# A graph attention layer on one core: first stage in another order with more row buffers, and an end with scores pair by pair

## The chip, the core and the metric

The kernel runs on one core of a Trainium2 chip. The metric is the time of one execution on the device, in microseconds, lower is better. The core has five engines that run beside each other, each through its own list of instructions in order: TensorE (PE; its weight loads are shown as PEld), VectorE (DVE), ScalarE (ACT), GpSimd (POOL) and SyncE (SP), which here only issues DMAs. ACT and POOL issue DMAs too.

## The reference

One layer of a graph network with 12,500 nodes, 212,500 edges sorted by their destination, 128 features and 8 heads of 16. The layernorm has no scale and no offset:

```python
h0 = maximum(layernorm(x), 0)
q = (h0 @ Wq.T + bq).reshape(N, 8, 16)
k = (edge_attr @ Wk.T + bk).reshape(-1, 8, 16)
v = (h0 @ Wv.T + bv).reshape(N, 8, 16)
qs, qd = q[src], q[dst]
in_m, out_m, diag_m = sum(qs * k, -1), sum(qd * k, -1), sum(qs * qd, -1)
score = (segment_softmax(in_m * SCALE, dst) + segment_softmax(out_m * SCALE, dst)
         + segment_softmax(diag_m * SCALE, dst)) * edge_weight ** lam
h = segment_sum(score[..., None] * v[dst], dst)
out = x + leaky_relu(h.reshape(N, 128) @ Wo.T + bo, 0.1)
```

Since v depends on the destination alone, the scores are summed for each node first, and v is multiplied once per node.

## The kernel before

**First stage.** x is held in SBUF as 98 tiles of 128 nodes (`xq`), loaded in runs by SP. It is worked off in 25 turns of four tiles: DVE measures (`bn_stats`, L897, then five small operations for the sums, L903 to L908), ACT takes the root (L912), DVE inverts (L916, L917), ACT rectifies (L927), PE turns the tile (L934), ACT copies it (L936), PE multiplies by Wq (L942), DVE adds the bias (L945), and SP stores q to a table in DRAM (L946), `q_table`. For eight of the 25 turns a split of q in three bf16 terms is made here and stored as well (a second view of the same table): `term_1` casts (ACT, L957), `less_1` subtracts it from q in place (DVE, L960), `term_2` casts the rest (ACT, L963), `term_3` subtracts again (DVE, L967). The other 17 turns' terms are made in the main loop, where the rest is formed by two matmuls (L1514, L1515). A dictionary `side` puts other small jobs on turns: the destinations' conversion and differences (`cast_dst`, `mark`, `edges_3`), weights (`turn_ws`), and so on. Every instruction's place on its engine is fixed by the program's own order (`pin`).

**Rows of the sources.** Edges are in 416 blocks of 512: five streams, with 83 groups of one block each, plus a short last one of 20 edges ("few"). Each block needs q of 512 source nodes, gathered by POOL with four indirect DMAs into a buffer `qq` of which there are `QQ` = 22. For the first 20 blocks (`RAW`) it gathers rows of x instead, which need no finished table, and the layernorm and the product with Wq are done on the gathered rows (`raw_measure` with `bn_stats` at L981, `raw_rectify` L714, and the rest in the first stage for `SOON` = 4 blocks, in the loop for the others, with a bias add at L1561). The later blocks gather from `q_table` (L702), which must be whole. `LOOK` = 20 is how many blocks ahead the loop gathers; the first three from the table, and then the rows of the few (`gather_few`, L730), are issued before the loop.

**Main loop.** Per block: PE turns the edge features (L1222), multiplies by Wk (L1229, L1231), spreads q of the destination nodes by a one-hot matrix (L1239); ACT copies (L1224, L1242); DVE makes three products (L1250 to L1252) and reduces to logits (L1253). `logits_few` (L1291 to L1307) does the same for the short block, at the seventh block. Per group: running maxima by scans on DVE (L1313 to L1343), powers (L1363, L1364), a product with the weights (L1375), and `to_rows`: sums of the powers per destination, by PE with a selection matrix (L1403), copied by ACT (L1408) and put into the `sums` tables in DRAM by SP (`put_rows`, L1419). `to_rows` handles three streams in one matmul: 126 columns of weights, 144 moving, of which the three blocks on the diagonal are used; eight of them per group. Edge features come by one DMA of 1280 KB per group (`fetch_edges`), in two buffers.

**Nodes and the end.** Behind the blocks, pairs of units of 256 nodes are finished: `scores` (L1112 to L1118, among them a reciprocal), `weigh` by v (L1178), the product with Wo (L1168, L1170), x added (L1194, L1195), the result stored (L1201). After the last block the remaining scans, powers and rows follow, then the remaining pairs (`rest`, five of them): their sums are loaded (L1143 on SP, L1145 on ACT), second parts added (L1732), scores made for all in one go over 432 columns, and then each pair is weighed, projected and stored.

Of the kernel before, what the change touches and what calls it, by code (L numbers as in the profile page):

```python
# [472 lines left out]
def ordered_path(ctx: ExitStack, tc: tile.TileContext, flag, x, src, dst, edge_attr, edge_weight,  # L473
# [143 lines left out]
    LOOK, QQ, RAW, SOON, DRAIN = 20, 22, 20, 4, 12  # L617
    FIRST, REST = 3, 5
    AHEAD, IDX = LOOK + FIRST, 7
# [31 lines left out]
    def fetch(t):  # L651
# [5 lines left out]
        if t < G:  # L657
# [7 lines left out]
        _, base_v[t] = nc.values_load_multi_w_load_instructions(  # L665
            places[0:1, t, 0:S], engines=[mybir.EngineType.SP], min_val=0, max_val=N - 1,
            skip_runtime_bounds_check_because="the indices of nodes are below N")
        st[t] = dict(relb=relb, far=far)
# [10 lines left out]
    def fetch_edges(t):  # L679
        if t < G:  # L680
            ea = eas[t] = load.tile([P, S, JN * F], F32, name="ea")
            pin(nc.sync.dma_start(
                ea, edge_attr[:end * BE, :].rearrange("(s b p j) f -> p s b (j f)", s=S, b=G, p=P)
                [:, :, t, :]))
# [62 lines left out]

    with tc.tile_pool(name="prep", bufs=1) as prep, \
# [5 lines left out]
        pin(nc.sync.dma_start(lam_sb, lam[None, :].to_broadcast([RW, 1])))  # L754
        w_in = prep.tile([P, 4, F], F32, name="w_in")
        pin(nc.sync.dma_start(w_in[:, 0, :], Wq))
        load_sources(0)
# [25 lines left out]
        for t in range(1, 3):  # L783
            load_sources(t)
        load_x(runs[2:])
        for t in range(3, IDX):
            load_sources(t)
        rows_in(weight, edge_weight.rearrange("e o -> (e o)"), nc.sync)
        b_row = prep.tile([1, 3, F], F32, name="b_row")
        for i, b in enumerate((bv, bk, bo)):  # L790
            pin(nc.sync.dma_start(b_row[:, i, :], b[None, :]))
# [3 lines left out]
        for s in range(S):  # L795
            at = s * G * BE
            pin(nc.sync.dma_start(bases[:, :, s:s + 1], dst[None, at:at + G * BE + 1:BE, None]))
# [13 lines left out]
        for i, w in enumerate((Wv, Wk, Wo)):  # L811
            pin(nc.scalar.dma_start(w_in[:, i + 1, :], w))
# [19 lines left out]
        def of_tile():  # L832
            return prep.tile([P, RC], BF, name="of", tag="of", bufs=2)[:RW]
# [22 lines left out]
        def edges_3():  # L856
            base_c = prep.tile([RW, RB], F32, name="base_c")
            pin(nc.vector.tensor_copy(base_c, dst_f[:, 1:RC + 1:BE]))
            rel_b = got["rel_b"] = of_tile().rearrange("r (a e) -> r a e", a=RB)
            for a in range(RB):  # L860
# [30 lines left out]

        def statistics(rows, *to):

            n = len(rows)
            stats = node.tile([P, CH, 6], F32, name="stats", bufs=1)[:, :n]
            for i, row in enumerate(rows):
                pin(nc.vector.bn_stats(stats[:, i, :], row))  # L897
            return sum_up(stats, n, *to)

        def sum_up(stats, n, *to):  # L900
            sums3 = node.tile([P, 3, CH], F32, name="sums3", bufs=4)[:, :, :n]
            total, apart, sq = sums3[:, 0], sums3[:, 1], sums3[:, 2]
            pin(nc.vector.tensor_add(total, stats[:, :, 1], stats[:, :, 4]))  # L903
            pin(nc.vector.tensor_sub(apart, stats[:, :, 1], stats[:, :, 4]))
            pin(nc.vector.tensor_add(sq, stats[:, :, 2], stats[:, :, 5]))
            pin(nc.vector.scalar_tensor_tensor(apart, apart, F / 4.0, apart, op0=ALU.mult,
                                               op1=ALU.mult))
            pin(nc.vector.tensor_add(sq, sq, apart))  # L908
            return *to, total, sq
# [166 lines left out]
        for g in range(-2, GN):  # L1076
# [9 lines left out]
            if g == -2:  # L1086
                for of in range(RAW):
                    gather(of)
# [702 lines left out]
```

## Time and profile before

| | |
|---|---|
| time, median of three executions | 2201.93 us (2199.54 to 2204.43) |
| profiled execution, its own time | 2203.34 us |
| its span in the profile | 2201.5 us |
| granted TensorE clock, mean | 0.796 |
| DVE busy | 2050.1 us, 93% |
| PE busy | 1779.5 us, 81% |
| POOL busy | 1586.5 us, 72% |
| ACT busy | 1372.0 us, 62% |
| DMA | 355.66 MB, 162 GB/s in the mean |

In rows of the timeline, the first number is the start in microseconds from the start of the span, the second the time busy; then engine, line, operation, output and inputs, how many were merged into the row, and in brackets how long the engine had been idle and what ended that. An engine's name with a q (SPq) is an issue of a DMA. In rows of groups, the columns after the bar are busy microseconds, mean nanoseconds of one, and idle time ahead with what ended it.

### The profile page before, as it was taken

How to read it: one execution, taken by the hardware profiler on the slowest of the kernel's cores; microseconds unless marked ns; L12 is line 12 of the kernel's file. 1: busy time of each engine (PE TensorE's matmuls, PEld its weight loads, DVE VectorE, ACT ScalarE, POOL GpSimd, SP SyncE). 2: the span in 40 equal slices, each digit the busy share in tenths (PEclk: the TensorE clock that was granted, in tenths of full speed). 3: DMA queues.
4: the chain of work that ended last, by engine and by line, in shares of the span. 5: the costliest groups of instructions: out<-in, count | busy, mean ns of one | idle time of the engine just before them, and what ended most of it. 6: DMA issues, size and time to landing. Idle time of an engine off the chain costs nothing.

```text
span 2201.5 us, 36690 instructions
## 1 busy us (share of the span) xinstructions
PE 1779.5 (81%) x10812; PEld 1418.5 (64%) x10812; DVE 2050.1 (93%) x2893; ACT 1372.0 (62%) x2555; POOL 1586.5 (72%) x1676
## 2 busy tenths in 40 slices
PE   4677888877887888888888888888888978888785
PEld 2565766666666666666766766766666767666664
DVE  6877999999999999999999999999999999999994
ACT  4777656665666566666656666666666656666671
POOL 7746777777777777777777777777777777777750
PEclk8788778787788778877878787787878787787887
DMA  8585456556646555655555565565555555555531
GB/s 227 168 252 159 145 150 181 158 162 177 169 148 189 165 161 154 187 162 164 157 169 154 144 186 149 156 171 151 151 167 162 154 170 155 150 171 158 156 99 58
DMA packets 373744, 355.66 MB, mean 162 GB/s; under 512 B 187698, under 2 KB 293437, under 8 KB 373327
## 3 DMA queue, kind: packets, MB, share of 16 engines
q1 hardware_dynamic: 304493, 237.91, 37.1%
q0 software_dynamic: 53184, 108.92, 17.8%
q10 hardware_dynamic: 15856, 6.39, 1.2%
q8 instruction: 87, 1.43, 0.3%
q14 instruction: 124, 1.02, 0.2%
HBM read 320.83 MB, written 32.17 MB: 160 GB/s over the span
## 4 chain that ended last, share of the span: by engine, by line
DVE 50%; PE 14%; DMA 11%; issue 4%; ACT 3%; POOL 1%; DVEq 1%; SPq 0%; ACTq 0%; POOLq 0%
DVE lT L1253 18%; DMA qq<-q_table,sources 11%; DVE prod L1250 7%; DVE prod L1252 7%; DVE prod L1251 7%; DVE m L1343 4%; PE k_ps L1231 4%; DVE l_ps L1313 3%; PE w_ps L1403 2%; PE eT_ps L1222 2%; DVE back L1363 1%; POOL qq L702 1%; PE m_ps L1355 1%; PE k_ps L1229 1%; DVE back L1375 1%
## 5 line engine op out<-in xcount | busy, mean ns | idle before, releaser
L702 POOL DMA_INDIRECT qq<-q_table,sources x1580 | 1498.2, 948 | 520.1 <-issue 219.1
L1253 DVE TENSOR_REDUCE lT<-prod 128x96 f32<-128x1536 f32 x415 | 727.4, 1753 | 14.3
L1231 PEld LDWEIGHTS k_ps<-wk,eT 128*128 128x128 f32 x3320 | 505.6, 233 | 201.2 <-issue 199.9
L1231 PE MATMUL k_ps<-wk,eT 128*128 128x128 f32 x3320 | 597.2, 335 | 0.7 <-ACT eT L1224 0.7
L1242 ACT COPY qd<-qd_ps 128x512 f32<-128x512 f32 x415 | 244.4, 589 | 138.7 <-DVE prod L1252 133.3
L1222 PE MATMUL eT_ps<-ident,ea 128*128 128x128 f32 x1660 | 310.3, 319 | 18.5 <-ACT eT L1224 16.1
L1364 ACT ACTIVATE back<-back 128x480 f32<-128x480 f32 x83 | 50.1, 604 | 416.8 <-DVE back L1363 416.8
L693 ACT ACTIVATE relb<-relb,before 126x512 bf16<-126x512 bf16 x415 | 303.4, 731 | 0.0
L1250 DVE TENSOR_TENSOR prod<-qq,qd_ps 128x512 f32<-128x512 f32 x412 | 279.0, 677 | 14.6 <-ACT qd L1242 9.1
L1239 PE MATMUL qd_ps<-win,oh 126*128 126x128 bf16 x1660 | 189.5, 245 | 124.2 <-DVE prod L1250 95.4
L1252 DVE TENSOR_TENSOR prod<-qd,k_ps 128x512 f32<-128x512 f32 x415 | 281.7, 679 | 0.0
L1251 DVE TENSOR_TENSOR prod<-qq,k_ps 128x512 f32<-128x512 f32 x412 | 279.7, 679 | 0.0
L1224 ACT COPY eT<-eT_ps 128x512 f32<-128x512 f32 x415 | 239.7, 578 | 62.6 <-PE eT_ps L1222 53.6
L1222 PEld LDWEIGHTS eT_ps<-ident,ea 128*128 128x128 f32 x1660 | 232.6, 165 | 60.0 <-ACT eT L1224 41.6
L694 ACT ACTIVATE oh<-relb 126x512 bf16<-126x512 bf16 x415 | 261.4, 630 | 13.2
L1239 PEld LDWEIGHTS <-oh 126*128 126x128 bf16 x1660 | 151.9, 112 | 148.2 <-issue 138.2
L1229 PE MATMUL k_ps<-b,ones 3*128 3x512 bf16 x415 | 186.7, 450 | 73.0 <-DVE prod L1252 70.9
L1403 PE MATMUL w_ps<-back,sel 128*126 128x144 f32 (+1 forms) x1344 | 212.6, 319 | 28.0 <-ACT sel L1393 12.6
L1403 PEld LDWEIGHTS w_ps<-back,sel 128*126 128x126 f32 (+1 forms) x1344 | 202.3, 219 | 34.4 <-ACT sel L1393 15.8
L1355 PE MATMUL m_ps<-ident,m 120*128 120x120 f32 x332 | 83.4, 400 | 85.4 <-DVE m L1343 80.8
L1355 PEld LDWEIGHTS m_ps<-ident,m 120*128 120x128 f32 x332 | 56.4, 217 | 104.1 <-DVE m L1343 67.4
L1343 DVE TENSOR_TENSOR_SCAN m<-far,head,l_ps 120x512 f32<-120x512 bf16 x81 | 102.9, 1271 | 0.0
(222 smaller groups left out, 1770.1 us busy)
## 6 DMA issues: line engine op xcount, KB each, us to landing
ea<-in_edge_attr_dram SPq DMA_DIRECT2D x83, 1280.0 KB
relb<-rel_d SPq DMA_DIRECT2D x83, 630.0 KB
qq<-q_table,sources POOLq DMA_INDIRECT x1580
win<-q_table SPq DMA_DIRECT2D x415, 31.5 KB
far<-far_d SPq DMA_DIRECT2D x84, 120.2 KB
q_table<-q SPq DMA_DIRECT2D x24, 384.0 KB
sums<-rows SPq DMA_DIRECT2D x412, 7.9 KB
q_table<-xq SPq DMA_DIRECT2D x24, 256.0 KB
```

Of the source, the lines that this page charges most:

```text
L693: pin(nc.scalar.activation(d, d, AF.Abs, bias=before[:K3]))
L694: pin(nc.scalar.activation(oh, d, AF.Relu, bias=1.0, scale=-1.0))
L702: rows = pin(nc.gpsimd.indirect_dma_start(out=qq[:, j, :], out_offset=None, in_=x if g < RAW else q_table, in_offset=bass.IndirectOffsetOn ...
L1222: pin(nc.tensor.transpose(eT_ps[:, j, :], eas[g // S][:, g % S, j * F:(j + 1) * F], ident))
L1231: pin(nc.tensor.matmul(k_ps[:, j, :], eTs[g][:, j, :], wk, start=False, stop=(j == JN - 1)))
L1239: pin(nc.tensor.matmul(qd_ps[:, j, :], ohs[g][:, j * P:(j + 1) * P], d["win"][:, s, :], start=(j == 0), stop=(j == JN - 1)))
L1242: pin(nc.scalar.copy(qds[g], qd_ps))
L1250: pin(nc.vector.tensor_mul(prod[:, :, 1, :], qqs[g], q_ps[g]))
L1251: pin(nc.vector.tensor_mul(prod[:, :, 0, :], qqs[g], ks[g]))
L1252: pin(nc.vector.tensor_mul(prod[:, :, 2, :], qds[g], ks[g]))
L1253: pin(nc.vector.tensor_reduce(lTs[t][:, :, s, :], prod.rearrange("p j i (h d) -> p j (i h) d", d=DIM), AX.X, ALU.add))
L1403: pin(nc.tensor.matmul(w_ps[:, i].rearrange("p s c -> p (s c)"), d["sel"][:n, j, lo:lo + 3, :].rearrange("p s w -> p (s w)"), d["back"][:n ...
```

## The change

It edits four places.

- **Buffers and order of loads.** `LOOK` 20 to 26, `QQ` 22 to 28, `SOON` 4 to 3, `IDX` 7 to 8; `RAW` stays at 20, so nine blocks (36 gathers) and not three are gathered from the table ahead of the few's rows and the loop. Edge features come by block (256 KB) into six buffers. SP loads x first, then the destinations, then the rest; Wv, Wk and Wo move from ACT's to SP's queue, biases, bases and index loads become jobs on turns. The tile `of` has one buffer in place of two.
- **First stage.** The sums take four operations in place of five; measuring is spread evenly, six `bn_stats` a turn; jobs move to other turns (`cast_dst` from turn -1 to 1). The raw rows are measured four blocks at a time; the last four (blocks 16 to 19) in the main loop. `less_1` is gone: the rest of q is formed by PE in PSUM.
- **to_rows.** One matmul for each stream and tile: 20 per group, 42 columns of weights and 48 moving; the copy by ACT is 42 x 240.
- **The end.** Scans, powers and rows of the last three groups interleaved; the last group's rows are put by ACT's queue; sums loaded in merged DMAs (SP for the first parts, ACT for the second); second parts added by DVE for the first pair and by POOL for the others; scores pair by pair, each followed by its weighing and projection.

```diff
-    LOOK, QQ, RAW, SOON, DRAIN = 20, 22, 20, 4, 12
+    LOOK, QQ, RAW, SOON, DRAIN = 26, 28, 20, 3, 12
-    AHEAD, IDX = LOOK + FIRST, 7
+    AHEAD, IDX, EDGES = LOOK + FIRST, 8, 6
...
-    def fetch_edges(t):
-        if t < G:
-            ea = eas[t] = load.tile([P, S, JN * F], F32, name="ea")
+    def fetch_edges(g):
+        if g < end:
+            ea = eas[g] = load.tile([P, JN * F], F32, name="ea", bufs=EDGES)
...
         load_x(runs[:1])
+        load_sources(0)
+        load_x(runs[1:2])
         pin(nc.sync.dma_start(bq_all, bq[None, :].to_broadcast([P, F])))
-        load_x(runs[1:2])
+        load_x(runs[2:8])
+        load_sources(1)
+        load_x(runs[8:])
         rows_in(dst_r[:, 1:RC + 1], dst, nc.sync)
...
-            return prep.tile([P, RC], BF, name="of", tag="of", bufs=2)[:RW]
+            return prep.tile([P, RC], BF, name="of", tag="of")[:RW]
...
-        def less_1(i):
-            pin(nc.vector.tensor_sub(q_of(i), q_of(i), q3s[i][:, :, 0, :]))
-
         def term_2(i):
-            pin(nc.scalar.copy(q3s[i][:, :, 1, :], q_of(i)))
+            rest = rests[i] = prep_ps.tile([P, JN, F], F32, name="t_ps")
+            pin(nc.tensor.matmul(rest, ident, q_of(i), start=True, stop=False))
+            pin(nc.tensor.matmul(rest, minus_b, q3s[i][:, :, 0, :], start=False, stop=True))
+            pin(nc.scalar.copy(q3s[i][:, :, 1, :], rest))
...
             if g == -2:
-                for of in range(RAW):
+                for of in range(3 * S):
                     gather(of)
             aside(g)
             if g == 9:
                 fetch_few()
+                for of in range(3 * S, RAW):
+                    gather(of)
         for g in range(RAW, AHEAD):
             gather(g)
         gather_few()
...
-            w_ps = small([3 * W, 2, 3, 2 * H3], "w_ps")
-            for i, (lo, _) in enumerate(trios):
+            w_ps = small([W, S, 2 * H3], "w_ps")
+            for s in range(S):
                 for j in range(JN):
-                    pin(nc.tensor.matmul(w_ps[:, i].rearrange("p s c -> p (s c)"),
-                                         d["sel"][:n, j, lo:lo + 3, :].rearrange("p s w -> p (s w)"),
-                                         d["back"][:n, j, lo:lo + 3].rearrange("p s i c -> p (s i c)"),
-                                         start=(i == 0 and j == 0), stop=(i == 1 and j == JN - 1)))
+                    pin(nc.tensor.matmul(w_ps[:, s, :], d["sel"][:n, j, s, :],
+                                         d["back"][j][:n, s].rearrange("p i c -> p (i c)"),
+                                         start=(s == 0 and j == 0), stop=(s == S - 1 and j == JN - 1)))
...
+            raw_last(g - 3)
             raw_add(g + SOON - 2)
             raw_product(g + SOON - 1)
...
-        scores_of(ab, score[:, :ab.shape[1]])
...
-                rest[r].weigh(rest[r].held)
+                scores_of(ends_ab[:, r * JN:r * JN + of.n], of.score[:, :of.n])
+                of.weigh(of.held)
+                of.turn(small([P, JN, P], "node_ps"))
+                of.project_o(of.held)
```

`raw_last(g)` takes, for g from 0 to 3, four `bn_stats` of one of the last four raw blocks; at 4 the sums and the root, at 5 the inversion.

More of the change, by code (lines that the diff above doesn't have):

```diff
@@ L1724, in ordered_path @@
         last_pair.turn(small([P, JN, P], "node_ps"))
+        hold(rest[0], "eT_ps")
         last_pair.project_o(small([P, JN, F], "node_ps"))
+        for which, q in ((0, nc.sync), (1, nc.scalar)):
+            for r, of in enumerate(rest):
+                of.load_last(ends_ab[:, r * JN:r * JN + of.n] if which == 0 else of.more, q, which)
+        for of, name in zip(rest[1:], ("k_ps", "qd_ps", "qd_ps", "k_ps")):
+            hold(of, name)
         last_pair.add_x(nc.vector)
         last_pair.store()
-        ab = ends_ab[:, :sum(of.n for of in rest)]
+        score = scan.tile([P, len(rest) * JN, HEADS], F32, name="end_score", bufs=1)
@@ L1742, in ordered_path @@
             if 0 <= r - 2:
-                rest[r - 2].project_o(small([P, JN, F], "node_ps"))
                 rest[r - 2].add_x(nc.vector)
```

316 lines of the change are left out of this document (170 added, 146 removed).

## The prediction

> **What bounds the kernel now.** I read the windows first, cut at the kernel's own stages: 54.6 us is where the sixth turn of the first stage starts, 134.7 where the loop over blocks does its first product, 2137.9 where its last reduce ends.
>
> ```profile
> core 0: us, PE busy (x) PEld busy (x) DVE busy (x) ACT busy (x) POOL busy (x), PEclk, DMA share, GB/s
> 0.00:54.60 54.60, 22.41 (x83) 16.24 (x83) 32.94 (x160) 22.13 (x54) 41.59 (x47) 0.83 0.86 227
> 54.60:134.70 80.10, 53.58 (x291) 43.02 (x292) 62.88 (x230) 58.14 (x139) 41.37 (x43) 0.80 0.60 186
> 134.70:2137.90 2003.20, 1664.63 (x10246) 1329.71 (x10246) 1924.82 (x2458) 1276.39 (x2335) 1503.52 (x1588) 0.80 0.57 162
> 2137.90:2201.50 63.60, 38.93 (x196) 29.54 (x194) 29.52 (x48) 15.34 (x28) 0.00 (x0) 0.69 0.18 55
> ```
>
> The loop is VectorE's (DVE): 1924.8 of 2003.2 us, 96%. Per group of five blocks it takes 2003.2 / 83 = 24.1 us. The other 198 us belong to no engine: in the first window the DMA engines are the busiest (0.86), in the second and the last every engine has holes. The edit is mostly in these three windows.
>
> Second, GpSimd's (POOL's) gathers in the timeline, and the one row of the waits that tells whether DVE wants them:
>
> ```profile
> 134.31 0.94 POOL L702 DMA_INDIRECT qq<-q_table,sources  x1 [26.24 <-DMA win<-q_table]
> 135.56 0.94 POOL L702 DMA_INDIRECT qq<-q_table,sources  x1 [0.30 <-issue]
> ...
> 149.29 0.89 POOL L730 DMA_INDIRECT qq<-q_table,few_i  x1 [0.30 <-issue]
> ...
> 2130.28 0.95 POOL L702 DMA_INDIRECT qq<-q_table,sources  x1 [0.30 <-issue]
> DVE prod L1250 <- DMA qq<-q_table,sources: 0.6, 2, 0.4
> ```
>
> One gather starts every 1.25 us. 395 or 396 blocks of four are 1975-1980 us of gathers; the stretch from 134.31 to 2131.2 is 1997, so POOL idled some 20 us in it. DVE waited 0.6 us for rows in the whole run. POOL starts 20 blocks ahead and ends nearly level (last gather 2131.2, last reduce 2137.9): it is close to being the bound, yet it isn't.
>
> Third, the first stage's timelines: what kept it from starting.
>
> ```profile
> 8.88 0.87 DVE L897 BATCH_NORM_STATS2 stats<-xq 128x6 f32<-128x128 f32 x4 [2.25 <-DMA xq<-in_x_dram]
> 16.04 0.87 DVE L897 BATCH_NORM_STATS2 stats<-xq 128x6 f32<-128x128 f32 x4 [4.87 <-DMA xq<-in_x_dram]
> 50.68 0.69 DVE L960 TENSOR_TENSOR xq<-xq,q 128x512 f32<-128x512 f32 x1 [8.71 <-DMA q_table<-xq]
> 21.33 1.88 ACT L849 CAST dst_r<-dst_r 104x2049 f32<-104x2049 int32 x1
> 27.08 1.63 ACT L927 ACTIVATE xq<-xq,shift,inv 128x128 f32<-128x128 f32 x4
> 37.01 1.64 ACT L927 ACTIVATE xq<-xq,shift,inv 128x128 f32<-128x128 f32 x4
> 40.01 1.66 ACT L927 ACTIVATE xq<-xq,shift,inv 128x128 f32<-128x128 f32 x4
> 54.67 1.63 ACT L927 ACTIVATE xq<-xq,shift,inv 128x128 f32<-128x128 f32 x4
> 47.89 2.19 SPq L946 DMA_DIRECT2D q_table<-xq  x4
> ```
>
> Rectifies that follow one another are 3.0 us apart (37.01, 40.01). The three steps from the third (27.08) to the sixth (54.67) take 27.6 us, 18.6 more than that: x had come late before them (4.87), ACT's and DVE's steps for dst and raw rows lie between (27.08 to 37.01), and at 40.01 all stops. There less_1 (L960) writes its result over q in xq, so it waits until that q is stored; its store was issued at 47.89 only, behind all loads of SP's queue.
>
> **First stage, forecast -18 us (from -8 to -27).** x goes first now. x is 12500 x 128 x 4 = 6.4 MB. The first window ran 227 GB/s at a share of 0.86, so 264 GB/s is my estimate of what the queues can carry; the raw gathers take 128 x 512 B per 1.25 us, 52 of that. 6.4 MB / 212 GB/s = 30 us. dst stands behind x and takes 0.85 MB / 212 = 4 us more if it gets no share before. ScalarE's (ACT's) cast of dst stands in order after the third rectify, so it begins at 30 to 34 and lasts 1.9; three rectifies on, at 3.0 apart, the sixth is at 38 to 42 and not at 54.7: 13 to 17 us, 15 taken.
>
> The other 80.1 us keep their chain of turns. Out go less_1 (8 x 0.6 = 4.8 us of DVE), the statistics of raw blocks 16 to 19 (below, 4.2), some 2 us of sums in fewer calls and the waits on q's stores. In come 16 matmuls for the rest of q:
>
> ```profile
> L1514 PE MATMUL rest_ps<-q_in,ident 128*128 128x512 f32 (+1 forms) x34 | 28.2, 929 | 0.0
> L1515 PE MATMUL rest_ps<-q,minus_b 128*128 128x512 bf16 (+1 forms) x17 | 9.0, 527 | 0.0
> ```
>
> Each rest is two records of the first row (its starts are about 0.5 apart) and one of the second, 1.0 + 0.4 = 1.4 us; 8 are 11 us on TensorE (PE), whose 53.6 us become 65 of 80. DVE falls from 62.9 to 52. There is one new wait: dst's `of` tile has one buffer and not two, so edges_3 on DVE waits for the store of `far`, which is queued on SP behind two stores of q; behind it stand that turn's add of the bias, its statistics, and ACT's next rectify. The 8.71 above is the nearest row, 3 to 5 us my guess. Work gone 11, of which about half was on the chain (DVE was 79% busy), less 3: a gain of 3. Sum -18, the loop starts at 116 or 117. The upper bound of the gain has 15 + 12; the lower has 13 and a loss of 5 to PE.
>
> **Loop, forecast +11 (from +3 to +20).** gather_few is moved behind nine blocks of gathers (36) and not three (12). What waits for its rows:
>
> ```profile
> 171.03 1.75 DVE L1253 TENSOR_REDUCE lT<-prod 128x96 f32<-128x1536 f32 x1
> 175.49 0.47 DVE L1299 TENSOR_TENSOR few_prod<-qq,few_ps 20x128 f32<-20x128 f32 x2 [2.71 <-DMA qq<-q_table,sources]
> 51.29 0.86 DVE L981 BATCH_NORM_STATS2 raw_stats<-qq 128x6 f32<-128x128 f32 x4
> 52.19 0.17 DVE L903 TENSOR_TENSOR sums<-raw_stats 128x8 f32<-128x8 f32 x1
> ```
>
> Before, DVE ends the reduce at 172.78, 38 us after the first gather, and waits 2.7. Now the few rows are asked for 36 x 1.25 = 45 us after it, take 2.4 for two gathers and some 2.5 to land: 50. DVE gets there at 38 plus 3 x 0.87 of the moved statistics, plus the 2.7: about 44. It stops for 6; nothing of the block's later work passes it, since each engine's order is fixed. Moved statistics: 4 x 0.87 + 4 x 0.17 + the inversion = 4.5, plus one more bias add (0.6): 5. Sum +11. The lower bound, +3, has the few rows landing 5 us sooner and some statistics in waits; the upper, a stop twice as long and ACT late behind it.
>
> 28 row buffers in place of 22 let POOL run further ahead. DVE waits 0.6 us for rows, so they buy at most that: 0. Edge features go from one 1280 KB DMA per group to five of 256 KB with six buffers. Row for an issue on SP: the four of 47.89 take 2.19, 0.55 each; four more a group are 2.2 us of a queue with gaps, beside puts of rows and loads of windows. The lead falls from a group to five blocks, 24 us: 0, up to +5.
>
> A rule that speaks against it: the Trainium skill, "DMA: Bandwidth & Descriptors", section Measured, asks for at least 1 MiB per DMA, and its fit gives 2.6 us for 256 KB, 5.0 for 1280 KB (estimates), so five cost 13.0 in place of 5.0. The DMA share of 0.57 has room for that in 24.1 us; by the page the sum would have +0 as well, and +8 x 83 only with no lead at all.
>
> The unnamed part is larger: to_rows is 20 narrow matmuls (42 columns of weights, 48 moving) and not 8 wide ones (126 and 144).
>
> ```profile
> 1211.47 2.23 PE L1403 MATMUL w_ps<-back,sel 128*126 128x144 f32 x16
> 1213.53 0.60 PE L1273 MATMUL l_ps<-ident,lT 128*120 128x128 f32 x4
> 1216.13 0.41 PE L1281 MATMUL h_ps<-ident,lT 16*120 16x16 f32 x4
> 1216.46 0.66 PE L1222 MATMUL eT_ps<-ident,ea 128*128 128x128 f32 x4
> PE qd_ps L1239 <- DVE prod L1250: 95.4, 63, 3.6
> PE k_ps L1229 <- DVE prod L1252: 70.9, 96, 0.8
> ```
>
> Starts: 2.06 us for 16 records is 0.129 each; 0.33 for four with 16 columns is 0.082. Between them, 48 columns give 0.094; 40 records take 3.8 us, +1.7 a group. It lies on PE beside DVE's work; PE's waits for DVE are 166.3 / 83 = 2.0 us a group. So 0, and from 0.102 us a record on ((2.06 + 2.0) / 40) DVE starts to wait. The Trainium skill, "TensorE: Matmul & The Clock Gate", section Back-to-back issue gap, has 62 ns a matmul where N is up to 64 and decode is in software: 40 x 0.062 = 2.5 (an estimate). By that the cost is 0 too, and the third case below has next to no chance; the row of 0.082 already contradicts it for matmuls with weight loads, so I keep the case.
>
> **End, forecast -8 (from 0 to -13).**
>
> ```profile
> 2139.75 0.75 DVE L1115 RECIPROCAL ab<-ab 128x96 f32<-128x96 f32 x1
> 2151.31 6.31 PE L1403 MATMUL w_ps<-back,sel 128*126 128x144 f32 x48 [1.19 <-DVE back L1375]
> 2170.35 0.70 DVE L1194 TENSOR_TENSOR node_ps<-h,node_ps 128x512 f32<-128x512 f32 x1 [14.97 <-ACT h L1189]
> 2171.69 1.95 DVE L1732 TENSOR_TENSOR ends_ab<-ends_ab,qq 128x384 f32<-128x384 f32 x4
> 2175.19 2.85 DVE L1115 RECIPROCAL ends_ab<-ends_ab 128x432 f32<-128x432 f32 x1
> 2179.40 0.69 DVE L1178 TENSOR_TENSOR qq<-eT_ps,end_score 128x512 f32<-128x512 f32 x1
> 2185.38 0.70 DVE L1194 TENSOR_TENSOR node_ps<-qq,node_ps 128x512 f32<-128x512 f32 x1 [4.10 <-ACT qq L1189]
> ```
>
> Between 2171.7 and 2179.4, 7.7 us, DVE makes all scores before the first weigh. Pair by pair the first needs one add (0.5) and one set of scores at the small shape, about 1.9 (the reciprocal is 0.75 of it): the first weigh comes 5 us sooner. The other scores fall in part into DVE's next wait (4.10), but cost more calls, which gives back 2 or 3. to_rows begins group by group, and the last group's puts go over ACT's queue while SP's are still landing; merged loads save issues: 3 to 5 of the 15 us. PE's 60 narrow matmuls end no later than the 24 wide. Sum -8.
>
> **Sum.** -18 + 11 - 8 = -15 on the profiled execution's 2203.3 (span 2201.5): 2188.3. It stands 1.4 above the median of the three runs, so 2187.
>
> **Rivals.** Second case: the first stage hardly gains. x may be no sooner (SP's queue was as full) or PE's 11 us decide the turns: -7 + 11 - 5 = -1, 2201. For it: the first window's DMA share is 0.86; against: the 18.6 us between steps aren't x, and the wait of 8.7 loses its cause.
>
> Third case, slower: narrow matmuls price above 0.102 us a record. At the wide row's 0.129, 5.2 us a group exceed the slack by 1.1, x 83 = +91: 2278; at 0.11 it is 0.3 x 83 = +27: 2214. Against it: 16 columns took 0.082.
>
> Fourth case: POOL, not DVE, sets the last third; with a longer lead its 20 idle us go too: 2167. Against it: 0.6 us of waits. That the added row buffers do nothing is in the forecast.
>
> **Chances.** Forecast 0.60, second 0.16, third 0.14, fourth 0.10. The measurement tells 0.2%, 4.4 us: below 2197.5 is faster, above 2206.3 slower. Forecast: 0.58 faster, 0.02 same. Second: 0.04, 0.06, 0.06 slower. Third: 0.01 same, 0.13 slower. Fourth: faster. Sums 0.72, 0.09, 0.19. Range 2168 to 2210: the sums of the bounds on the forecast's side (2172 to 2199 alone), the second case, and the near end of the third.
>
> **What would show it.** Right: first L1250's counterpart near 117, POOL's first gather from q_table just before it; few_prod with a wait of 5 to 9 us; loop of about 2014; w_ps's 40 records in 3.5 to 4.1 us and PE's waits for DVE smaller by 1.7 a group; end of 55. Wrong: the loop starting after 125; DVE waits for qd or k of over 40 us in all; DVE's waits for ea; a loop shorter than 2003.

## The result, and the profile after

The changed kernel takes 2193.85 us (2192.16 to 2194.26, five executions) against 2201.93 for the kernel before in the same comparison (2199.54 to 2204.53): a ratio of 0.9961, 95% interval 0.9950 to 0.9971, some 8 us less. The profiled execution has a span of 2192.1 us, 9.4 less than before.

Six of the runs below were made on two other chips, on which the kernel before took 2717.8 and 2719.3 us; of those only the end of the kernel and the step into the loop are compared with other runs.

The windows of the profile after are cut at the loop's first product and its last reduce, as before; the cut at 41.6, inside the rectifies, only parts the early stretch.

```profile
core 0: us, PE busy (x) PEld busy (x) DVE busy (x) ACT busy (x) POOL busy (x), PEclk, DMA share, GB/s
0.00:41.60 41.60, 13.90 (x46) 9.56 (x47) 17.80 (x86) 14.65 (x33) 30.64 (x38) 0.80 0.92 243
41.60:125.30 83.70, 69.04 (x340) 48.79 (x340) 64.01 (x230) 62.60 (x149) 50.97 (x52) 0.83 0.71 209
125.30:2134.90 2009.60, 1653.25 (x12202) 1310.58 (x12202) 1929.38 (x2481) 1273.09 (x2342) 1502.77 (x1588) 0.80 0.61 162
2134.90:2192.10 57.20, 41.76 (x268) 30.51 (x266) 33.29 (x70) 15.58 (x30) 3.12 (x3) 0.65 0.20 61
```

| stage | before | after | difference | forecast |
|---|---|---|---|---|
| up to the loop's first product | 134.7 | 125.3 | -9.4 | -18 |
| loop | 2003.2 | 2009.6 | +6.4 | +11 |
| after the last reduce | 63.6 | 57.2 | -6.4 | -8 |
| span | 2201.5 | 2192.1 | -9.4 | -15 |

All three signs are as forecast; each size is smaller, the first by half.

**First stage.** ACT's timeline after, at the point where dst is cast:

```profile
16.07 1.64 ACT L932 ACTIVATE xq<-xq,shift,inv 128x128 f32<-128x128 f32 x4
...
37.27 1.90 ACT L879 CAST dst_r<-dst_r 104x2049 f32<-104x2049 int32 x1 [19.10 <-DMA dst_r<-in_dst_dram]
39.08 1.64 ACT L932 ACTIVATE xq<-xq,shift,inv 128x128 f32<-128x128 f32 x4
41.88 1.65 ACT L932 ACTIVATE xq<-xq,shift,inv 128x128 f32<-128x128 f32 x4 [0.49 <-DVE shift L771]
44.42 1.65 ACT L932 ACTIVATE xq<-xq,shift,inv 128x128 f32<-128x128 f32 x4
```

x is there early: the fourth rectify ends at 17.7 and not at 28.7. Then ACT stands 19.1 us for dst, with all further rectifies behind the cast in its list. The seventh comes at 44.42 (54.67 before), and from there to the loop it takes 80.9 us (80.0 before). The prediction and the expectations call these two the third and the sixth: they count the first two rectifies, which stand in one row of eight activations, as one. It is the same rectify in all kernels.

The 80.9 us are divided otherwise than before. The rows from the last bias add to the loop's first product, first of the kernel before, then of the changed one:

```profile
126.55 0.42 DVE L945 TENSOR_TENSOR xq<-q_ps,bq_all 128x256 f32<-128x256 f32 x1
132.42 0.59 PE L1239 MATMUL qd_ps<-win,oh 126*128 126x128 bf16 x4 [4.73 <-DMA win<-q_table]
134.73 0.69 DVE L1250 TENSOR_TENSOR prod<-ends_ab,qd_ps 128x512 f32<-128x512 f32 x1 [0.62 <-ACT qd L1242]
...
121.84 0.41 DVE L950 TENSOR_TENSOR xq<-q_ps,bq_all 128x256 f32<-128x256 f32 x1
125.34 0.69 DVE L1267 TENSOR_TENSOR prod<-ends_ab,qd_ps 128x512 f32<-128x512 f32 x1 [0.62 <-ACT qd L1259]
```

From the seventh rectify to the last add it takes 77.4 us and not 71.9, from the last add to the first product 3.5 and not 8.2. So 4.7 of the stage's 9.4 us come at its exit, where PE had stood 4.73 us for the first window of q.

**Loop.** The rows of the few, in POOL's and DVE's timeline:

```profile
169.88 0.90 POOL L734 DMA_INDIRECT qq<-q_table,few_i  x1 [0.30 <-issue]
...
172.14 0.28 DVE L1316 TENSOR_TENSOR few_prod<-qq,few_ps 20x128 f32<-20x128 f32 x1 [5.39 <-DMA qq<-q_table,few_i]
173.46 0.28 DVE L1316 TENSOR_TENSOR few_prod<-qq,few_ps 20x128 f32<-20x128 f32 x1 [1.04 <-DMA qq<-q_table,few_i]
```

The gather for the few starts 45.0 us after the first one from the table, as forecast, and DVE stops for 6.4 us (2.7 before). DVE's busy time in the loop grows by 4.6 us, the moved statistics. These make 8.3; waits elsewhere shrink by 1.9.

**to_rows.** One group in PE's timeline:

```profile
1209.59 1.90 PE L1427 MATMUL w_ps<-back,sel 128*42 128x48 f32 x40
1211.42 0.65 PE L1290 MATMUL l_ps<-ident,lT 128*120 128x128 f32 x4
```

From start to start 1.83 us for 40 records, 0.046 each, where I had put 0.094; eight wide matmuls had 2.06. These are also the medians of the loop's groups; the longest take 3.4 us narrow and 4.0 wide. The narrow form is no longer than the wide one.

**End.** DVE's timeline of the last pairs:

```profile
2161.28 0.69 DVE L1207 TENSOR_TENSOR node_ps<-h,node_ps 128x512 f32<-128x512 f32 x1 [7.28 <-ACT h L1202]
...
2163.34 0.56 DVE L1771 TENSOR_TENSOR ends_ab<-ends_ab,qq 128x384 f32<-128x384 f32 x1 [0.64 <-DMA qq<-sums]
...
2165.24 0.75 DVE L1123 RECIPROCAL ends_ab<-ends_ab 128x96 f32<-128x96 f32 x1
...
2167.45 0.69 DVE L1191 TENSOR_TENSOR qq<-eT_ps,end_score 128x512 f32<-128x512 f32 x1
```

The first of these weighs starts 32.6 us after the last reduce (2134.85), before it was 41.5 us (2179.40 against 2137.87): 8.9 sooner, of which some 2.5 are given back by the later pairs' calls. Of the 8.9, 5.3 are won already at the first add of second parts (28.5 us after the last reduce, before 33.8), and 3.6 between that add and the first weigh (4.1 us, before 7.7).

A part of the 5.3 may come from a move that the list of the change doesn't name. PE's turn of the last pair stood behind the products with Wv of four further pairs (from 2157.46 on); now it stands ahead of them. PE's rows, before and after:

```profile
2163.97 0.60 PE L1162 MATMUL node_ps<-ident,h 128*128 128x128 f32 x4
...
2154.06 0.66 PE L1175 MATMUL node_ps<-ident,h 128*128 128x128 f32 x4
```

That is 26.1 and 19.2 us after the last reduce. No run tested this move alone.

### The profile page after: what moved, and what is told of

It reads as the page before. It is cut to its first block, busy times and chain, and to the rows that moved or that the text cites. A ratio compares the mean times of both kernels' runs of the same rounds, so it can differ in the third digit from the quotient of the medians.

```text
span 2192.1 us, 41487 instructions
## 1 busy us (share of the span) xinstructions
PE 1777.9 (81%) x12852; PEld 1399.4 (64%) x12852; DVE 2044.5 (93%) x2865; ACT 1365.9 (62%) x2552; POOL 1587.5 (72%) x1679
## 4 chain that ended last, share of the span: by engine, by line
DVE 49%; PE 16%; DMA 7%; issue 5%; ACT 4%; POOL 2%; DVEq 1%; SPq 1%; ACTq 0%; POOLq 0%
DVE lT L1270 18%; DVE prod L1267 7%; DVE prod L1269 7%; DVE prod L1268 6%; DMA qq<-q_table,sources 6%; PE k_ps L1248 4%; DVE m L1361 4%; PE w_ps L1427 3%; PE eT_ps L1239 2%; DVE l_ps L1330 2%; POOL qq L706 2%; DVE back L1382 1%; PE k_ps L1246 1%; PE qd_ps L1256 1%; PE node_ps L1183 1%
## 5 line engine op out<-in xcount | busy, mean ns | idle before, releaser
L1270 DVE TENSOR_REDUCE lT<-prod 128x96 f32<-128x1536 f32 x415 | 727.4, 1753 | 14.3
L1248 PEld LDWEIGHTS k_ps<-wk,eT 128*128 128x128 f32 x3320 | 496.5, 229 | 198.0 <-issue 196.9
L1248 PE MATMUL k_ps<-wk,eT 128*128 128x128 f32 x3320 | 587.1, 331 | 0.6 <-ACT eT L1241 0.6
L1239 PE MATMUL eT_ps<-ident,ea 128*128 128x128 f32 x1660 | 310.2, 319 | 27.1 <-ACT eT L1241 23.8
L1427 PE MATMUL w_ps<-back,sel 128*42 128x48 f32 x3320 | 196.5, 230 | 26.5 <-ACT sel L1419 12.8
L1427 PEld LDWEIGHTS w_ps<-back,sel 128*42 128x42 f32 x3320 | 186.0, 140 | 41.5 <-ACT sel L1419 16.3
```

Of the source, the lines that this page charges most:

```text
L1239: pin(nc.tensor.transpose(eT_ps[:, j, :], eas[g][:, j * F:(j + 1) * F], ident))
L1248: pin(nc.tensor.matmul(k_ps[:, j, :], eTs[g][:, j, :], wk, start=False, stop=(j == JN - 1)))
L1270: pin(nc.vector.tensor_reduce(lTs[t][:, :, s, :], prod.rearrange("p j i (h d) -> p j (i h) d", d=DIM), AX.X, ALU.add))
L1427: pin(nc.tensor.matmul(w_ps[:, s, :], d["sel"][:n, j, s, :], d["back"][j][:n, s].rearrange("p i c -> p (i c)"), start=(s == 0 and j == 0), ...
```

## The experiments

The kernels here start from the changed one, unless said otherwise.

**1. The cast of dst later.**

```diff
-        side = {0: [load_b], 1: [cast_dst, load_bases], 3: [mark], 4: [store_far], 5: [(edges_3, (0, 1)), load_w],
-                6: [(edges_3, (2, 3))], 7: [store_rel], 8: [biases], 9: [near_due],
-                13: [(fetch, 0)], 18: [(fetch, 1)], 20
+        side = {0: [load_b], 1: [load_bases], 7: [cast_dst], 9: [mark, near_due], 10: [store_far],
+                11: [(edges_3, (0, 1))], 5: [load_w], 12: [(edges_3, (2, 3))], 13: [store_rel], 8: [biases],
+                15: [(fetch, 0)], 18: [(fetch, 1)], 20
```

> The changed kernel with ACT's cast of dst at turn 7 in place of turn 1, and what follows from it (mark, the store of far, edges_3, the store of rel, the first fetch, near_due) two to six turns later. In the changed kernel ACT stood 19.1 us at the cast (18.2 to 37.27) and the sixth rectify came at 44.4. Theory A, the wait for dst alone made the first stage longer than forecast: the sixth rectify comes at 25 to 30, the loop's first product at 111 to 118 in place of 125.3, the time is 7 to 14 us below the changed kernel's 2193.9. Theory B, x itself was late (the DMA engines were 0.92 busy): the sixth rectify stays after 38, DVE waits for x in bn_stats, the loop starts no more than 3 us sooner, the time is within 3 us of 2193.9.

2196.62 us (2194.53 to 2198.55), ratio to before 0.9970 (0.9959 to 0.9981). Neither theory holds whole. The seventh rectify did come early, at 23.8, and x was not late; yet the loop's first product is at 125.2. ACT's timeline ahead of the cast, where the time went:

```profile
33.53 0.33 ACT L766 ACTIVATE inv<-sums,eps 128x18 f32<-128x18 f32 x1
54.27 0.62 ACT L962 CAST q<-xq 128x512 bf16<-128x512 f32 x1 [20.41 <-DMA q_table<-q]
```

A stop of 20.4 us takes the place of the 19.1: the third split needs one of two buffers, and the first split's store is issued by SP at 50.58 only, behind dst, weights, biases and bases.

**2. dst loaded earlier.**

```diff
         load_sources(1)
-        load_x(runs[8:])
         rows_in(dst_r[:, 1:RC + 1], dst, nc.sync)
         pin(nc.sync.dma_start(dst_r[1:, 0:1], dst[RC - 1:(RW - 1) * RC:RC, None]))
+        load_x(runs[8:])
```

> The changed kernel with dst's loads issued ahead of the last seven runs of x, the cast left at turn 1. Theory A, dst behind all of x is what held ACT: dst lands near 20 in place of 37, ACT's stop at the cast falls from 19.1 to under 6 us, the sixth rectify comes at 28 to 33, the time is 5 to 12 us below 2193.9. Theory B, the DMA engines set it: what dst gains x loses, DVE waits for x at the later turns by about as much, the time is within 3 us of 2193.9.

2193.10 us (2192.99 to 2196.98), ratio 0.9955 (0.9941 to 0.9968). As far as the cast goes theory A is right: the stop falls to 3.0 us and the seventh rectify comes at 27.96. The time doesn't follow; the loop starts at 124.5. Here it is DVE that stops next, at the tile that lost its second buffer:

```profile
54.36 1.25 DVE L893 TENSOR_SCALAR of<-dst_r,base_c 104x512 bf16<-104x512 f32 x2 [17.98 <-DMA far_d<-of]
```

In the changed kernel this wait, which I had put at 3 to 5 us, is 1.45; it grows to 18 as soon as DVE gets there early, since the store stands in the same queue of SP.

**3. SP's queue cleared as well.** On top of experiment 1: weight and lam are loaded by ACT's queue at the start, biases and bases as jobs of turns 5 and 6, Wv, Wk and Wo at turn 7.

```diff
-        pin(nc.sync.dma_start(lam_sb, lam[None, :].to_broadcast([RW, 1])))
+        pin(nc.scalar.dma_start(lam_sb, lam[None, :].to_broadcast([RW, 1])))
...
-        rows_in(weight, edge_weight.rearrange("e o -> (e o)"), nc.sync)
+        rows_in(weight, edge_weight.rearrange("e o -> (e o)"), nc.scalar)
...
+        side = {5: [load_b], 6: [load_bases], 7: [cast_dst, load_w], 9: [mark], 10: [store_far],
+                11: [(edges_3, (0, 1)), near_due], 12: [(edges_3, (2, 3))], 13: [store_rel], 14: [biases],
...
```

> The changed kernel with the cast of dst at turn 7 and its followers later, as in the run with the late cast, and SP's queue cleared between x and q's first stores: weight and lam load by ACT's queue at the start, biases and index bases as jobs of turns 5 and 6. With the late cast alone ACT reached the third split at 34 and then stood 20.4 us until the first split's store, issued at 50.6 behind those loads. Theory A, SP's queue set the first stage: that stop falls under 6 us, the loop's first product comes at 108 to 116 and the time is 2178 to 2187. Theory B, the DMA engines carry no more (0.9 to 1.1 busy to 30 us and 0.8 to 0.9 after 90): stores and loads land later by what they are issued sooner, the loop starts after 121, the time is 2190 to 2196.

> [...] Theory A, SP's queue set the first stage: ACT's stop of 20.4 us at the third split falls under 6 us, the loop's first product comes at 108 to 116, the time is 2178 to 2187. Theory B, the DMA engines or POOL's raw gathers (to 107) set it: the loop starts after 121, the time is 2190 to 2196.

The first run was on the chip with 2717.8 us for the kernel before and settles nothing here (2766.14 us, ratio 1.0179). The second: 2194.70 us (2192.16 to 2195.99), ratio 0.9966 (0.9952 to 0.9979). The stop at the third split falls to 10.0 us, not under 6, and the loop starts at 124.4. The edit has a price of its own at the start: ACT stands until its queue has issued the loads that it took over, and the seventh rectify comes at 31.1, later than the 23.8 of run 1.

```profile
14.87 0.27 ACT L908 COPY wq<-t_ps 128x128 f32<-128x128 f32 x1 [11.17 <-DMA lam_sb<-in_L_gnn_lam_dram]
```

The time is where theory B put it; but in this kernel q was ready sooner than that. SP's and POOL's timelines at the end of the stage, and DVE's last bias add:

```profile
108.51 0.42 SPq L974 DMA_DIRECT2D q_table<-q  x1
108.98 0.54 SPq L686 DMA_DIRECT2D ea<-in_edge_attr_dram  x1
109.61 0.78 SPq L951 DMA_DIRECT2D q_table<-xq  x1
117.36 0.44 SPq L680 DMA_DIRECT2D win<-q_table  x1
117.91 0.39 SPq L951 DMA_DIRECT2D q_table<-xq  x1
...
120.95 0.34 SPq L951 DMA_DIRECT2D q_table<-xq  x1
113.94 0.69 DVE L950 TENSOR_TENSOR xq<-q_ps,bq_all 128x512 f32<-128x512 f32 x1 [0.87 <-PE t_ps L855]
...
117.16 0.42 DVE L950 TENSOR_TENSOR xq<-q_ps,bq_all 128x256 f32<-128x256 f32 x1
123.96 0.94 POOL L706 DMA_INDIRECT qq<-q_table,sources  x1 [17.39 <-DMA win<-q_table]
```

SP stands from 110.4 to 117.36 at the first load of a window of q, which reads the splits' table and so waits until their last store (108.51) has landed (5.9 us are put down to that store); four stores of q stand behind it, three of them with their data ready (the adds end before 115). The last is issued at 120.95, and POOL's gathers can start at 123.96. The last add is 4.7 us sooner than in the changed kernel (121.84), the first gather only 1.0.

Two comparisons show what this is worth. First, the last add varies by itself: in runs 5, 6 and 7, whose turns are those of the changed kernel, it comes at 121.00, 118.95 and 119.91, so it can't be said how much of the 4.7 us is the edit's. Second, the step from the last add to the loop's first product does not vary: it is 3.5 us in the changed kernel and in runs 2, 5, 6 and 7, but 6.5 in run 1 and 7.2 in run 3. By that SP's stop takes 3.0 and 3.7 us from these two.

The changed kernel itself, in DVE's, SP's and POOL's timelines, and one window of it:

```profile
121.84 0.41 DVE L950 TENSOR_TENSOR xq<-q_ps,bq_all 128x256 f32<-128x256 f32 x1
122.28 0.33 SPq L951 DMA_DIRECT2D q_table<-xq  x1
124.92 0.94 POOL L706 DMA_INDIRECT qq<-q_table,sources  x1 [17.50 <-DMA qq<-in_edge_attr_dram]
60.00:90.00 30.00, 23.85 (x109) 15.37 (x107) 29.24 (x115) 20.66 (x51) 22.95 (x24) 0.83 0.61 185
```

Here the last store follows its add at once: SP's stop is over before it matters, and the turns themselves set the start. The window shows a possible reason why they come no sooner, which no run tested: from 60 to 90 us DVE is busy for 29.24 of 30 (28.48 before the change, 28.47 and 29.21 in runs 1 and 3). A lead won before 60 us meets an engine without holes there, and most of what is left of it (the last add is 3.1 us sooner in run 1, 4.7 in run 3) ends at SP's stop.

**4. The windows after the last store.** This was to settle what SP's stop costs, alone (with LOOK 20) and together with 3.

```diff
         for k in range(S):
-            beside(20 + k, fetch_rows, 0, [k])
+            beside(GN, fetch_rows, 0, [k])
```

> The kernel with LOOK 20 and 22 row buffers, and the five loads of q's windows for the first group issued on SP after the last of q's stores, in place of between the last five. In the changed kernel SP stood before the first window load from about 110 to 116.2 (it waits for the last split's store to land), with four stores of q behind it, and the loop's first product came at 125.3 (122.5 with LOOK 20). Theory A, that stop sets the end of the first stage: the last store of q is issued at 117 to 119 and not 119.4 or later, the loop starts 2 to 5 us sooner than 122.5 and the time is 2183 to 2186. Theory B, the last turns of ACT and DVE set it (the last bias add near 119): the loop starts within 1.5 us of 122.5, or later by the windows' own loads, and the time is within 2 us of 2187.8.

> LOOK 20 and 22 row buffers, the cast of dst at turn 7 with its followers later, SP's queue cleared between x and q's first stores (weight and lam by ACT's queue), and the window loads after the last store of q. With the cleared queue but the windows between the stores, the last bias add came near 115 and yet the loop began at 124.4. Theory A, each removed stop hid behind the next and all three together show: the loop starts at 113 to 119, the time is 2178 to 2184. Theory B, the DMA engines (0.8 to 0.9 busy after 90) land the last stores no sooner: the loop starts at 121 to 123, the time is 2186 to 2190.

2743.98 us (ratio 1.0085, 1.0071 to 1.0098) and 2746.86 us (1.0096, 1.0080 to 1.0111), both on the chip where the kernel before takes 2719.26. There the loop starts at 194.4 and 191.8, so what SP's stop costs in time stays open. One thing can be read: from the last add to the loop's first product both take 5.3 us, where the kernels of runs 6, 8 and 9 take 3.5 on the other of the two slower chips. Loaded behind the last store, the windows cost some 1.8 us of their own.

**5. The few's rows asked for first.**

```diff
-        for g in range(RAW, AHEAD):
+        for g in range(RAW, RAW + FIRST):
             gather(g)
         gather_few()
+        for g in range(RAW + FIRST, AHEAD):
+            gather(g)
```

> The changed kernel with gather_few issued after three blocks of gathers from the table, as before the change, and the other six blocks behind it. Theory A, the 36 gathers ahead of the few's rows hold DVE: few_prod's wait falls from 6.4 us to 0 to 2.7, the loop is 4 to 6 us shorter (2004 to 2006 in place of 2009.5), the time 2188 to 2190. Theory B, DVE's stop is filled later since it waits elsewhere for POOL or PE anyway: few_prod's wait falls, the loop stays within 1.5 us of 2009.5.

2194.46 us (2192.47 to 2195.06), ratio 0.9959 (0.9946 to 0.9973): no gain. The loop is 2007.7 us, between the theories. DVE's and POOL's timelines:

```profile
163.18 0.47 DVE L1318 TENSOR_TENSOR few_prod<-qq,few_ps 20x128 f32<-20x128 f32 x2 [2.71 <-PE few_ps L1315]
...
182.54 1.54 DVE L1605 TENSOR_SCALAR shows<-ends_ab 21x840 bf16<-21x840 f32 x1 [6.66 <-POOL ends_ab L1599]
181.27 1.24 POOL L1599 IOTA ends_ab<- 21x840 f32 x1
```

few_prod's wait is back at 2.7, waiting for PE and no longer for rows. The 24 extra gathers now stand ahead of the next thing that DVE needs of POOL, an index built by `iota`, and DVE waits 6.7 us for it.

**6. LOOK 20, 22 row buffers.** Three blocks of gathers ahead, so that both the few's rows and the index come early.

```diff
-    LOOK, QQ, RAW, SOON, DRAIN = 26, 28, 20, 3, 12
+    LOOK, QQ, RAW, SOON, DRAIN = 20, 22, 20, 3, 12
```

> The changed kernel with LOOK 20 and 22 row buffers as before; with that three blocks of gathers and not nine stand ahead of the few's rows and the loop's index builds on POOL. Theory A, more row buffers bring nothing and only put POOL's other jobs behind 24 more gathers: few_prod's wait falls to 2.7, no wait of DVE for POOL's index build (6.7 us where only the few's gathers were moved ahead), the loop is 4 to 7 us shorter than 2009.5 and the time 2187 to 2190. Theory B, the longer lead saves DVE stops late in the loop, where gathers are nearly level with their use: waits of DVE for rows of over 3 us appear after 1800, and the time stays within 2 us of 2193.9 or above.

> [...] Theory A, more row buffers bring nothing and put the few's rows and POOL's index build behind 24 more gathers: few_prod's wait falls to 2.7, no wait of DVE for the index build, the loop is 4 to 7 us shorter than 2009.5, the time 2187 to 2190. Theory B, the longer lead saves DVE stops late in the loop: waits for rows of over 3 us appear after 1800, the time is within 2 us of 2193.9 or above.

The first run was on the chip with 2717.8 us for the kernel before (2749.33 us, ratio 1.0103). The second: 2187.82 us (2186.50 to 2191.22), ratio 0.9940 (0.9926 to 0.9953), the fastest of all here. On the same chip run 3 took 2192.16 to 2195.99, so the two do not overlap. Theory A holds: the loop is 2003.1 us, 6.5 shorter. Only that is put down to the lead: the loop also starts 2.8 us sooner (122.5), about as in run 7 (123.4), whose first stage is the changed kernel's, and the end is 1.9 longer (59.1).

```profile
149.15 1.24 POOL L1597 IOTA ends_ab<- 21x840 f32 x1
...
161.84 0.47 DVE L1316 TENSOR_TENSOR few_prod<-qq,few_ps 20x128 f32<-20x128 f32 x2 [2.71 <-PE few_ps L1313]
DVE prod L1267 <- ACT qd L1259: 6.3, 6, 1.8
```

The index is built at 149 and not at 182; DVE's waits for qd fall too (11.4 us in the changed kernel), which pays for the moved statistics. DVE's waits for gathered rows are 0.4 us in all, also without the longer lead.

**7. to_rows with wide matmuls**, in the changed kernel: the two groups of three streams of before, eight matmuls a group.

```diff
-            w_ps = small([W, S, 2 * H3], "w_ps")
-            for s in range(S):
+            w_ps = small([3 * W, 2, 3, 2 * H3], "w_ps")
+            for i, (lo, _) in enumerate(trios):
                 for j in range(JN):
...
+                                         d["sel"][:n, j, lo:lo + 3, :].rearrange("p s w -> p (s w)"),
+                                         d["back"][j][:n, lo:lo + 3].rearrange("p s i c -> p (s i c)"),
```

> The changed kernel with to_rows as before: eight wide matmuls a group (126 columns of weights, 144 moving). In the changed kernel 40 narrow records of one group took 1.9 us, 16 wide ones of before 2.2. Theory A, PE's part lies beside DVE and the two cost the same: within 2 us of 2193.9, PE's waits for DVE's products unchanged near 171 us. Theory B, narrow records stretch PE where the clock is low and hold DVE at qd or k: wide is 3 to 15 us faster. Theory C, narrow is the cheaper one and PE's end of the kernel gains by it: wide is 2 to 4 us slower, in the end stage.

2193.23 us (2190.35 to 2193.64), ratio 0.9952 (0.9938 to 0.9965): theory A. The loop is 2008.7 us, 0.9 shorter, within what single profiles differ by: the loops of runs 1 to 3, which leave it alone, take 2009.9 to 2012.2.

**8. All scores in one go.**

```diff
+        whole = sum(of.n for of in rest)
+        scores_of(ends_ab[:, :whole], score[:, :whole])
         for r in range(len(rest) + 2):
...
-                scores_of(ends_ab[:, r * JN:r * JN + of.n], of.score[:, :of.n])
```

> The changed kernel with all scores of the last five pairs made in one go over 432 columns, after the second parts are added, as before. Theory A, the pairwise scores are what shortened the end: the first weigh comes 3 to 6 us later, the end stage is 60 to 62 us in place of 57.3. Theory B, pair by pair costs DVE as much in calls as it brings at the first weigh, and the gain lies in the rows and loads ahead: the end stage stays within 1.5 us of 57.3.

This ran on the chip with 2717.8 us for the kernel before (2769.38 us, ratio 1.0196). In the stretch after the last reduce the five other kernels that ran on the two slower chips take 57.0 to 58.5 us, the changed kernel on the usual chip 57.2; this one takes 64.8:

```profile
2700.45:2765.20 64.75, 43.35 (x268) 31.89 (x267) 28.58 (x47) 15.75 (x30) 3.08 (x3) 0.63 0.18 54
2733.43 1.06 DVE L1120 TENSOR_TENSOR ends_ab<-ends_ab 128x864 f32<-128x864 f32 x1 [3.78 <-POOL ends_ab L1771]
...
2739.15 0.69 DVE L1191 TENSOR_TENSOR qq<-eT_ps,end_score 128x512 f32<-128x512 f32 x1
```

The first weigh is at 38.7 us and not 32.6 after the last reduce. 3.8 of the 6.1 us is a wait for POOL's adds of the second parts, which pair by pair is hidden. In the changed kernel, then, scores in one go cost 6 to 8 us: theory A, with more than its 3 to 5. This is not their share of the change's gain. The kernel before made the adds by DVE in 1.95 us and had no such wait; from its first add to its first weigh it took 7.7 us, this run takes 10.1.

**9. The rest of q by DVE.**

```diff
-            rest = rests[i] = prep_ps.tile([P, JN, F], F32, name="t_ps")
-            pin(nc.tensor.matmul(rest, ident, q_of(i), start=True, stop=False))
-            pin(nc.tensor.matmul(rest, minus_b, q3s[i][:, :, 0, :], start=False, stop=True))
+            rest = rests[i] = q_of(i)
+            pin(nc.vector.tensor_sub(rest, rest, q3s[i][:, :, 0, :]))
```

> The changed kernel with the rest of q by DVE, in place in xq, as before the change, at the turns of the changed kernel; PE's 24 records of the rest are gone. Theory A, PE's added 11 us lie beside other work: the loop starts within 3 us of 125.3, the time within 3 us of 2193.9. Theory B, the second half of the stage hangs on PE (DVE waits 2.8 to 3.5 us for q from PE in the turns from 93 to 114): the loop starts 4 to 9 us sooner and the time falls by as much. Theory C, the store that less_1 waits for comes late on SP's queue again: a stop of DVE of 5 us or more at L960's counterpart, the loop starts 3 to 10 us later.

2767.59 us on the chip with 2717.8 us for the kernel before (ratio 1.0181, 1.0165 to 1.0198), where the first stage takes 190 us and more in every kernel profiled. Inconclusive: none of the three theories is tested by it.

## Why the prediction was right, and where its steps were not

**The sum.** -15 was forecast, -9.4 came in the profiles and -8 in the medians. The direction came from the first stage and the end, against a loss in the loop, as written. That the sum is off by only 5.6 us is in part luck: the first stage fell short by 8.6 and the end by 1.6, the loop's loss was put too high by 4.6, and half of the first stage's gain came from a place that the forecast doesn't name. The range's inner bounds, 2172 to 2199, are also narrower than what the bounds of the three terms add up to (some 2165 to 2214).

**First stage, the term that was mis-sized: -18 forecast, -9.4 measured.** Its first part, 15 us at the seventh rectify (the prediction's sixth), was 10.2. The step that fell short is the landing of dst: 30 to 34 us forecast from 264 GB/s, 37.27 measured. The window that holds it ran 243 GB/s at a share of 0.92, which is 264 at a full share again: the rate was right, the share was not full. Its second part, 3 us less over the remaining turns, was 5.5 more instead, up to the last bias add; the exit then took 4.7 less, and no term of the forecast has that. The moved window loads, now at turns 20 to 24 and not 22 to 25, are the likely reason for the shorter exit, since PE stood for a window there; no run on the faster chips tested it.

The experiments show that the method of the step failed, not only its figure: I counted the seventh rectify's lead as a gain of the stage, and it is not. With that rectify at 23.8, 28.0 and 31.1 in place of 44.4 the loop began at 125.2, 124.5 and 124.4; with the changed kernel's own turns it began at 124.5 and 123.4 in runs 5 and 7. Each stop that was taken away gave its time to the next: ACT at the third split's buffer (20.4 us, then 10.0), DVE at `of` (18.0), SP at the first window of q. I had named the queue of SP as "behind all loads" for the kernel before and did not follow that the stores still stand behind dst, weights and bases; nor did I follow the window loads, moved ahead of the last stores of q. That this stop takes 3.0 and 3.7 us in runs 1 and 3 is read from their timelines; no run without it settled it. The second case, a first stage that hardly gains, was nearer here than the forecast in size (-7), with other reasons than it gave: x was not late, and the rest's matmuls took 14 us on PE where it had 11, with DVE's waits for q after 93 us beside them; whether they cost anything stayed open.

**Loop: +11 forecast, +6.4 measured.** The moved statistics were forecast as 5, and DVE's busy time grew 4.6. The stop at few_prod was forecast as 6 on top of the 2.7 us that it waited before; it is 6.4 in all, so it grew by 3.7. Both ends of that wait came sooner than reckoned: DVE ends its reduce 41.8 us after the first gather (44 forecast, with the 2.7), the last of the few's rows is there at 48.5 (50 forecast). DVE's waits for q's split and for h shrank a little besides (23.2 to 22.8 and 2.9 to 1.8). Run 6 shows the larger part of the loss to be the longer lead: without it the loop is 2003.1, with the statistics in it.

**28 row buffers: 0 forecast.** Right about the gain, wrong about the price: they are what puts 24 gathers ahead of POOL's other jobs. The 6.5 us of loop between the changed kernel and run 6 are that price. The fourth case, POOL as the bound, has nothing for it.

**to_rows: 0 forecast, 0 measured** (run 7), though the record was mis-sized twofold (0.094 against 0.046). PE's waits for DVE, which were to fall by 1.7 us a group, did not: 171.4 us after, 166.3 before. The third case is excluded on the chips of the two profiles. 0.046 is also below the 62 ns that the prediction took from the Trainium skill's page "TensorE: Matmul & The Clock Gate", section Back-to-back issue gap. The page gives that figure for decode in software, and this trace doesn't show how the decode is done; it lies above the 25 ns that the page gives as the floor.

**Edge features by block: 0 forecast.** The loop shows no wait of DVE or PE for them of note, and the DMA share went from 0.57 to 0.61 at the same 162 GB/s. Breaking the rule of one MiB from the Trainium skill's page "DMA: Bandwidth & Descriptors", section Measured, costs nothing that shows here: that share is the only trace of the smaller transfers. The page measured its rule and the fit that the prediction used on DMAs issued by GpSimd, and these are issued by SP.

**End: -8 forecast, -6.4 measured.** Both reasons are there, and the split was nearly right. Rows and loads bring 5.3 us up to the first add, where I had 3 to 5, the last pair's turn moved ahead among them. Scores pair by pair bring 3.6 at the first weigh, where I had 5, and the calls give back 2.5, as forecast. So the pairs carry about 1 of the 6.4. Run 8 doesn't speak against that: its 6 to 8 us hold a wait for POOL's adds that the kernel before did not have.

## What to carry to other kernels

A wait at the head of a stage is worth only what the stage's last wait lets through: before counting an early lead as a gain, follow the lead to the stage's exit, and list every queue that its stores stand in. A deeper prefetch is not free even where buffers are: everything else on the issuing engine moves behind the added transfers, and one must look for who waits for that. Where several independent outputs come at the end, cutting a long chain by output starts the first one sooner, but the extra calls can give back most of it: here 2.5 of 3.6 us.

## What the runs showed of the hardware that was not expected

A record of a small float32 matmul with 42 columns of weights and 48 moving took 0.046 us from start to start, less than the 0.082 that records with 16 columns showed when they stood alone in groups of four. Perhaps the ends of those short groups made most of the 0.082; no run tested it.

On two chips the kernel before took 2717.8 and 2719.3 us, and six variants of the changed one 2744 to 2769, with DVE's operations as long as elsewhere (its reduce 1753 ns in the mean) and a granted TensorE clock of 0.73 to 0.75 in the variants' profiles (0.80 to 0.81 elsewhere). There the engines stand with nothing to wait for that the kernel names: "issue" is a wait for nothing that the profile shows, "remote" one for another core or an unknown queue. The waits of run 3 on the first of these chips:

```profile
POOL qq L706 <- remote: 219.6, 134, 6.8
DVE prod L1268 <- remote: 166.4, 72, 22.5
PE eT_ps L1239 <- issue: 137.8, 78, 6.2
```

On these chips all six variants were 0.9 to 2.0% slower than the kernel before, the three with LOOK 20 the least (0.9 to 1.0%; one of them ran on the first chip, two on the second). So the gain of the change may not carry over to every chip; the changed kernel itself was not run on them. The variants have about 41,500 instructions where the kernel before has 36,690, most of the difference from to_rows' narrow matmuls (run 7, with wide ones, has 37,455). One reading is that the engines there lack their instructions; no run tested it, and the cause stays open.
